# VectorE's order around the rotation of k and q: sums of exponentials moved beside the third norm's root, that norm's transpose moved behind k's cosines

## The chip, the cores and the metric

The kernel runs on one core of a Trainium2 chip. The metric is the device time in microseconds of one execution, lower is better; the time given for the kernel before is a median of 3 runs. A profile is one execution recorded by the hardware profiler. Its times are counted from the first instruction of the span. The engines are called PE (TensorE, the matrix engine; PEld are its weight loads), DVE (VectorE), ACT (ScalarE), POOL (GpSimd) and SP (SyncE, which here only issues DMAs).

## The reference, cut to what matters

Sixteen batch rows `b` of 128 positions by 512 features go through three residual blocks, all in float32:

```python
x = x + xattn(layernorm(x), ctx)      # ctx: 16 x 2048 x 512
x = x + attn(layernorm(x), ...)       # 16 heads of 32, causal, rotary
x = x + ffn(layernorm(x), Wr, A, Bw)  # + x's norm; 8 low-rank experts, top 2

def xattn(h, c):
    p = softmax(einsum('bld,bvd->blv', h, c), axis=-1)
    return einsum('blv,bvd->bld', p, c)

# in attn, for q and k of each head (the rotated half of each):
rot = stack((-x2, x1), axis=-1).reshape(x.shape)   # neighbours swapped, one negated
return x * cos + rot * sin
...
scores = where(causal, q @ k.T * scale, -inf); att = softmax(scores); y = (att @ v) @ Wc
```

The denominator of the first softmax is a sum over the 2048 context positions of the exponentials; the kernel makes it in pieces on VectorE.

## The kernel before

One batch row is one unit of work, and one pass of the loop `for b in range(B - 2)` (line 1134) works on several rows at once: it finishes the self-attention of row b (`inner`), does the experts of row b - 1 (`experts`), the scores of row b + 2 (`score`) and the weighted sum over the context of row b + 1 (`attend`). Each of these is a generator; `step(kind, b, n)` runs it to its next n `yield`s. So the order of `step` calls and the places of `yield` decide in which order instructions are issued.

Three things set the final order. PE's matmuls and all loads on a queue keep the program's order (`matmul`, `transpose`, `load`, lines 138 to 147). Instructions wrapped in `pinned` (line 151) keep it too, on their engine. The rest is placed by a scheduler when the program is built.

The stretch that the change touches lies around the rotation of k and q:

- `output` and `added` (lines 750 to 761) make the product `o` on PE and the new residual `x2` on VectorE, in the last step of `inner(b)`. There `layernorm(x2, "3_b")` (line 775) is called: `bn_stats` (tile `st`), `bn_aggr` (tile `mv`), the root on GpSimd (tile `rs`, two small instructions: add eps, then power), and the normalised `h` on VectorE (`norm_pieces`, line 186).
- `transposed` (line 263) turns `h` in blocks of 32 by 32 on VectorE into `blocks`; `send` writes them to DRAM (`there`) and `fetch` reads them back as `hT`, both on SP's queue. For the third norm this happens in the first step of `experts`, and its fetch is followed on that queue by the send and fetch of the first norm of another row.
- `rotated(n, t)` (line 653), for k and then q: `products` on PE; `shuffled` on VectorE, which swaps neighbours from PSUM into `kP` or `qP` (one tile in SBUF, tag `partner`, is used in turn by both); `sines` on GpSimd, which multiplies that tile by a table; `cosines` on VectorE, PSUM times a table, into `kT` or `qT`. `turned` (line 649) then adds the two on VectorE. `blocked` copies kT twice on ScalarE into `kb`. `compare` (line 673) multiplies qT by kb on PE, into the tiles called `pss_sc` and `pss_acc`.
- `score(b + 1)` (line 394) makes the sums of its exponentials meanwhile: `sums = sc0 + sc1`, then `+ sc2`, `+ sc3` (128 x 512 each), then `halved` (line 427), a fold of 128 x 256 and one of 128 x 128, then `across` (line 377), which begins with a transpose (`turned_den`) and ends as the reciprocal `rden`.

On PE the order of one pass around this place is: o of row b, k and q of row b + 1, one quarter of `av` (the weighted sum of row b + 2), `pss_sc`, `pss_acc`, the other three quarters, the scores `psc`, the experts' `mid` and `ffn`, then y, v and the next o.

Of the kernel before, what the change touches and what calls it, by code (L numbers as in the profile page):

```python
# [15 lines left out]
ALU = mybir.AluOpType  # L16
# [9 lines left out]
VC = V // 512  # L26
# [63 lines left out]
def perceiver_block(ctx: ExitStack, tc: tile.TileContext, io: dict, out: bass.AP):  # L90
# [60 lines left out]
    def pinned(ins):  # L151
        if not closing:
            tc.keep_in_program_order(ins)
# [55 lines left out]
    def layernorm(src, name, mix=False):  # L209
        h, pieces = norm_pieces(src, name, mix=mix)  # L210
        for piece in pieces:
            ins = piece()

            if ins is not None and name.startswith("1_") and piece is not pieces[1]:
                pinned(ins)
        return h
# [46 lines left out]
    def transposed(src, dst, name, by_tensor):  # L263
        n = src.shape[1] // P
        if by_tensor:
            for piece in tensor_pieces(lambda: src, dst, name, n):
                piece()
        else:
            blocks = p1.tile([P, 4, n, QD], F32, tag=f"blocks_{name[0]}", name=f"blocks_{name}")
            vector.transpose(blocks, src.rearrange("p (n q i) -> p q n i", n=n, q=4))  # L270
            ways[name] = blocks, dst


# [58 lines left out]
    scores, firsts, values, lasts, routes = {}, {}, {}, {}, {}  # L332
# [61 lines left out]
    def score(b):  # L394

        hT = p1.tile([P, 4, KC, QD], F32, tag="hT1" if b != 1 else "hT3", name=f"hT1_{b}")
        if b:
            h = layernorm(xs[b], f"1_{b}", mix=b == 1)
            yield
            transposed(h[:], hT, f"1_{b}", b == 1)  # L400
        else:
            first_norm(xs[b], hT)
            yield
        yield

        sc = p2.tile([P, VC, 4, S], F32, tag="sc", name=f"sc_{b}")
        mx = p1.tile([P, 4, S], F32, tag="mx", name=f"mx_{b}")
        for v, ct in enumerate(turned_cts.pop(b)):
            ps = bank(ps_sc, "sc", f"psc_{b}_{v}").rearrange("p (j t) -> p j t", j=4)
            for j in range(4):  # L410

                if v == VC - 1 and j == 3:
                    yield
                for c in range(KC):
                    matmul(
                        ps[:, j, :].rearrange("p (a i) -> p a i", a=4),
                        ct[:, c, j * P : (j + 1) * P], hT[:, :, c, :],
                        start=(c == 0), stop=(c == KC - 1),
                    )
            scalar.copy(sc[:, v], ps)  # L420

            if v:
                vector.tensor_tensor(mx, ps, mx if v > 1 else sc[:, 0], ALU.max)
            if v < VC - 1:
                yield

        def halved(t, op):
            vector.tensor_tensor(t[:, :2], t[:, :2], t[:, 2:], op)
            vector.tensor_tensor(t[:, 0], t[:, 0], t[:, 1], op)
            return t[:, 0]  # L430

        most = halved(mx, ALU.max)
        if b > 1:

            spread = p1.tile([P, 4, QD], F32, tag="spread", name=f"spread_{b}")
            peak = across(most, f"m_{b}", ALU.max, negate=True)
            for a in range(4):
                pinned(vector.transpose(
                    spread[a * QD : (a + 1) * QD], peak[:, :, None].to_broadcast([QD, 4, QD])
                ))  # L440
            for v in range(VC):
                pinned(vector.tensor_tensor(
                    sc[:, v], sc[:, v],
                    spread.rearrange("p j i -> p (j i)")[:, None, :].to_broadcast([P, 4, S]), ALU.add,
                ))
                if v < 2:
                    scalar.activation(sc[:, v], sc[:, v], AF.Exp)
            yield

            for v in range(2, VC):  # L450
                pinned(scalar.activation(sc[:, v], sc[:, v], AF.Exp))
            sums = p1.tile([P, 4, S], F32, tag="sums", name=f"sums_{b}")
            if b == B - 1:
                part = p2.tile([P, S], F32, tag="part", name=f"part_{b}")
                scores[b] = (sc, part)
                yield
                yield
                pinned(vector.tensor_tensor(sums, sc[:, 0], sc[:, 1], ALU.add))
                yield
                for v in range(2, VC):  # L460
                    pinned(vector.tensor_tensor(sums, sums, sc[:, v], ALU.add))
                named(
                    b, fold=lambda: vector.tensor_tensor(sums[:, :2], sums[:, :2], sums[:, 2:], ALU.add),
                    last_fold=lambda: vector.tensor_tensor(part, sums[:, 0], sums[:, 1], ALU.add),
                )
                yield
                return
            pinned(vector.tensor_tensor(sums, sc[:, 0], sc[:, 1], ALU.add))
            yield
            for v in range(2, VC):  # L470
                pinned(vector.tensor_tensor(sums, sums, sc[:, v], ALU.add))
            yield
            whole = across(halved(sums, ALU.add), f"den_{b}", ALU.add)
            vector.reciprocal(whole, whole)
            rden = p2.tile([P, 1], F32, tag="rden", name=f"rden_{b}")
            for a in range(4):
                vector.tensor_copy(rden[a * QD : (a + 1) * QD], whole[:, a : a + 1])
            scores[b] = (sc, rden)
            yield
            yield  # L480
            return
        yield

        tr = bank(ps_tr, "tr", f"tr_m_{b}")
        transpose(tr[:, :S], most, ident)
        nm = p2.tile([P, 1], F32, tag="nm", name=f"nm_{b}")
        vector.tensor_reduce(nm, tr[:, :S], AX.X, ALU.max, negate=True)
        diag = p1.tile([P, S], F32, tag="diag", name=f"diag_{b}")
        vector.tensor_scalar(diag, ident, nm, None, ALU.mult)
        yield  # L490
        spread = bank(ps_tr, "tr", f"spread_{b}")
        matmul(spread[:, :S], ones, diag, start=True, stop=True)
        for v in range(VC):
            vector.tensor_tensor(
                sc[:, v], sc[:, v], spread[:, None, :S].to_broadcast([P, 4, S]), ALU.add
            )
            scalar.activation(sc[:, v], sc[:, v], AF.Exp)
        part = p2.tile([P, S], F32, tag="part", name=f"part_{b}")
        scores[b] = (sc, part)
        yield  # L500
        sums = p1.tile([P, 4, S], F32, tag="sums", name=f"sums_{b}")
        pinned(vector.tensor_tensor(sums, sc[:, 0], sc[:, 1], ALU.add))
        yield
        for v in range(2, VC):
            pinned(vector.tensor_tensor(sums, sums, sc[:, v], ALU.add))

        def fold():
            vector.tensor_tensor(sums[:, :2], sums[:, :2], sums[:, 2:], ALU.add)

        def last_fold():  # L510
            vector.tensor_tensor(part, sums[:, 0], sums[:, 1], ALU.add)

        fold()
        last_fold()
        yield
# [62 lines left out]
    def inner(b):  # L578
# [179 lines left out]
        x2 = Later(p2, [P, D], tag="x2", name=f"x2_{b}")  # L758

        def added():  # L760
            vector.tensor_tensor(x2[:], banks["o"], x1[:], ALU.add)

        if b < B - 2:
            parts = [
                (project, kept), (lambda: rotated("k", kT),),
                (lambda: turned("k", kT), blocked), (lambda: rotated("q", qT),),
                (lambda: turned("q", qT),), (lambda: compare(0), lambda: compare(1)),
            ]
            parts += [(lambda group=group: weigh(group),) for group in range(4)]
            parts += [(weighted, held), (output, added)]  # L770
            for part in parts:
                for piece in part:
                    piece()
                if part[-1] is added:
                    lasts[b] = (x2, layernorm(x2, f"3_{b}"))
                yield
            return

# [280 lines left out]
    def step(kind, b, n=1):  # L1059
        if not 0 <= b < B:  # L1060
            return
        if (kind, b) not in gens:
            gens[kind, b] = kind(b)
        for _ in range(n):
            next(gens[kind, b])
# [68 lines left out]
    for b in range(B - 2):  # L1134
        if b + 3 < B:
            load_x(b + 3)
        step(inner, b)
        step(experts, b - 1)
        send(f"3_{b - 1}")
        fetch(f"3_{b - 1}")  # L1140
# [1 line left out]
            send(f"1_{b + 2}")  # L1142
            fetch(f"1_{b + 2}")
        step(inner, b, 3)
        step(score, b + 1, 2)
        step(attend, b + 1)
        step(inner, b)
        step(attend, b + 1)
# [29 lines left out]
        step(score, b + 3)  # L1178
        step(inner, b)
        step(score, b + 2)  # L1180


    y, z = B - 2, B - 1
# [60 lines left out]
```

## Time and profile before

| what | us |
|---|---|
| median of 3 runs (812.15 to 812.86) | 812.8 |
| the profiled execution, whole time | 812.06 |
| its span, first to last instruction | 810.3 |
| length of one pass of the loop (distance of two starts of `pss_sc`, 222.09 and 270.10) | 48.01 |
| POOL multiplying kP or qP by sines, one | 1.27 |
| VectorE, 128 x 512 float32, one (sums, cosines, additions) | 0.65 to 0.69 |
| VectorE, block transpose 128 x 512, one | 0.71 |
| mean DMA rate over the span, GB/s | 260 |

The granted TensorE clock was 1.0 throughout. How to read the timelines used below: each row is start, duration, engine, line, operation, the tile written and those read after an arrow, shapes and count; in square brackets the engine's idle time before it and whom it waited for. All instructions issued through the helpers have line L115 (vector, scalar, gpsimd), L139 (matmuls) or L147 (loads), so rows are told apart by their tiles. Consecutive instructions of one engine overlap a little in the records[...].

### The profile page before, as it was taken

To read this page: it belongs to the slowest core of one execution; us is meant where nothing else is said; L and a number is where in the kernel's file an instruction comes from. 1 tells how busy PE (TensorE), PEld (TensorE's weight loads), DVE (VectorE), ACT (ScalarE), POOL (GpSimd) and SP (SyncE) were. 2 spreads that over 40 slices of the span, in tenths; PEclk is the share of its full clock that TensorE was granted. 3 is DMA by queue.
4 is the path that set the end of the run, shared out by engine and by line. 5 is a ranking of instruction groups with operands and counts; after the bars stand their busy time and mean duration, and the time that the engine had idled before them with its cause. 6 is when DMAs were issued, how large, how long until landed. Compare 5 with 4: busy or idle time off the path is not lost.

```text
span 810.3 us, 14522 instructions
## 1 busy us (share of the span) xinstructions
PE 790.0 (98%) x5444; PEld 559.8 (69%) x5444; DVE 612.2 (76%) x1593; ACT 258.2 (32%) x772; POOL 146.4 (18%) x214
## 2 busy tenths in 40 slices
PE   9999999999999999999999999999999999999996
PEld 9946775768677586866758677576867757686554
DVE  2464779686886968789696878968688696866785
ACT  2232324232232413223241232423223241322452
POOL 1001010212111121211212121021211112121204
PEclk9999999999999999999999999999999999999999
DMA  9997394867949588593957859486794948755102
GB/s 374 417 395 313 121 382 166 333 259 237 373 145 373 198 299 323 189 403 138 360 228 287 332 171 399 168 313 262 251 365 148 381 182 321 288 194 209 40 2 79
DMA packets 76870, 211.06 MB, mean 260 GB/s; under 512 B 6400, under 2 KB 42624, under 8 KB 60416
## 3 DMA queue, kind: packets, MB, share of 16 engines
q10 hardware_dynamic: 15696, 113.32, 35.1%
q1 hardware_dynamic: 57168, 84.75, 29.3%
q0 software_dynamic: 3936, 12.07, 4.5%
q8 instruction: 43, 0.70, 0.3%
q14 instruction: 27, 0.22, 0.1%
HBM read 180.23 MB, written 29.88 MB: 259 GB/s over the span
## 4 chain that ended last, share of the span: by engine, by line
PE 79%; DVE 13%; POOL 4%; issue 3%; DMA 0%; POOLq 0%; ACT 0%; DVEq 0%
PE psc L139 28%; PE av L139 22%; PE v L139 7%; PE o L139 7%; DVE sums L115 2%; PE pss_sc L139 2%; POOL qP L115 2%; DVE kT L115 2%; PE y L139 2%; PE pss_acc L139 2%; PE ffn L139 2%; PE mid L139 2%; POOL rs L115 1%; PE k L139 1%; PE q L139 1%
## 5 line engine op out<-in xcount | busy, mean ns | idle before, releaser
L139 PEld LDWEIGHTS psc<-hT,ctxT 128*128 128x128 f32 x2048 | 232.3, 192 | 6.7 <-issue 3.6
L139 PE MATMUL psc<-hT,ctxT 128*128 128x128 f32 x2048 | 233.9, 275 | 0.0
L139 PE MATMUL av<-ctx,sc 128*128 128x512 f32 x512 | 227.3, 596 | 0.0
L139 PEld LDWEIGHTS av<-ctx,sc 128*128 128x128 f32 x512 | 94.4, 190 | 110.5 <-issue 110.5
L115 ACT ACTIVATE att<-att,nmx 128x128 f32<-128x128 f32 x256 | 99.3, 389 | 77.5 <-DVE nmx L115 75.7
L115 POOL TENSOR_SCALAR rs<-mv 128x1 f32<-128x1 f32 x47 | 10.6, 225 | 411.8 <-DVE g_top L115 217.6
L115 ACT COPY sc<-psc 128x512 f32<-128x512 f32 x64 | 37.3, 582 | 120.3 <-PE psc L139 120.3
L115 ACT ACTIVATE kb<-kT,cst 128x512 f32<-128x512 f32 (+1 forms) x34 | 36.1, 1111 | 109.7 <-DVE kT L115 109.7
L115 DVE TENSOR_SCALAR h<-x,mv,rs 128x512 f32<-128x512 f32 x47 | 26.6, 567 | 54.5 <-POOL rs L115 54.5
L139 PEld LDWEIGHTS k<-hT,w_k 128*128 128x128 f32 x512 | 59.6, 192 | 8.2 <-issue 7.5
L115 ACT ACTIVATE sc<-sc 128x512 f32<-128x512 f32 x64 | 38.2, 627 | 69.9 <-DVE sc L115 56.0
L139 PE MATMUL k<-hT,w_k 128*128 128x128 f32 x512 | 60.1, 275 | 0.0
L139 PE MATMUL q<-hT,w_q 128*128 128x128 f32 x512 | 60.0, 275 | 0.0
L139 PE MATMUL o<-w_c,yT 128*128 128x512 f32 x128 | 59.2, 605 | 0.0
L139 PE MATMUL v<-w_v,hT 128*32 128x512 f32 x520 | 59.0, 593 | 0.0
L139 PEld LDWEIGHTS q<-hT,w_q 128*128 128x128 f32 x512 | 58.5, 192 | 0.0
L115 ACT ACTIVATION_READ_ACCUMULATOR att<-att,nmx 128x1 f32 x256 | 47.9, 187 | 0.0
L139 PEld LDWEIGHTS o<-w_c,yT 128*128 128x128 f32 x128 | 23.0, 189 | 35.5 <-issue 34.7
L115 DVE TENSOR_TENSOR mx<-psc,mx 128x512 f32<-128x512 f32 x32 | 21.6, 675 | 33.5 <-ACT sc L115 33.5
L115 DVE TENSOR_TENSOR att<-att,rsm 128x512 f32<-128x512 f32 x64 | 43.4, 678 | 0.7
L115 DVE TENSOR_REDUCE nmx<-att 128x4 f32<-128x512 f32 x64 | 43.1, 675 | 1.0
L115 DVE TENSOR_TENSOR sc<-sc,spread 128x512 f32<-128x512 f32 x64 | 40.0, 686 | 3.8 <-PE spread L139 3.3
(157 smaller groups left out, 898.8 us busy)
## 6 DMA issues: line engine op xcount, KB each, us to landing
ctx<-in_ctx_dram ACTq DMA_DIRECT2D x56, 1024.0 KB, 9.6
ctxT<-in_ctxT_dram ACTq DMA_DIRECT2D x52, 1024.0 KB, 9.8
there_p<-pX SPq DMA_DIRECT2D x28, 512.0 KB, 3.5
pT<-there_p SPq DMA_DIRECT2D x28, 512.0 KB, 4.4
ctxT<-in_ctxT_dram SPq DMA_DIRECT2D x12, 1024.0 KB, 9.0
there<-blocks SPq DMA_DIRECT2D x42, 256.0 KB, 3.4
hT<-there SPq DMA_DIRECT2D x42, 256.0 KB, 3.1
ctx<-in_ctx_dram SPq DMA_DIRECT2D x8, 1024.0 KB, 10.5
```

What stands on the lines that cost most here:

```text
L115: ins = issue(*args, **kwargs)
L139: tc.keep_in_program_order(nc.tensor.matmul(*args, **kwargs))
```

## The change

The arithmetic and the instructions stay; their order on VectorE changes. In `score`, the sum of the third quarter moves up to the first, the fourth stands alone, and the two folds get a step of their own ahead of `across`. In the last step of `inner`, h of the third norm is put off: statistics and root are issued, then comes a `yield`, and h follows in an added step at the end of the pass. The transpose of h is pinned, and one step of `score(b + 1)` moves ahead of `experts(b - 1)`, so that the folds stand ahead of that transpose.

```diff
@@ transposed
-            vector.transpose(blocks, src.rearrange("p (n q i) -> p q n i", n=n, q=4))
+            turn = vector.transpose(blocks, src.rearrange("p (n q i) -> p q n i", n=n, q=4))
+            if name[0] == "3":
+                pinned(turn)
@@ score
             pinned(vector.tensor_tensor(sums, sc[:, 0], sc[:, 1], ALU.add))
-            yield
-            for v in range(2, VC):
-                pinned(vector.tensor_tensor(sums, sums, sc[:, v], ALU.add))
-            yield
-            whole = across(halved(sums, ALU.add), f"den_{b}", ALU.add)
+            pinned(vector.tensor_tensor(sums, sums, sc[:, 2], ALU.add))
+            yield
+            pinned(vector.tensor_tensor(sums, sums, sc[:, 3], ALU.add))
+            yield
+            part = halved(sums, ALU.add)
+            yield
+            whole = across(part, f"den_{b}", ALU.add)
...
-            yield
             yield
             return
@@ inner
-            vector.tensor_tensor(x2[:], banks["o"], x1[:], ALU.add)
+            pinned(vector.tensor_tensor(x2[:], banks["o"], x1[:], ALU.add))
...
-                    lasts[b] = (x2, layernorm(x2, f"3_{b}"))
+                    h, norm = norm_pieces(x2, f"3_{b}")
+                    for piece in norm[:3]:
+                        piece()
+
+                    yield
+                    pinned(norm[3]())
+                    lasts[b] = x2, h
                 yield
@@ the loop over b
         step(inner, b)
+        step(score, b + 1)
         step(experts, b - 1)
...
         step(inner, b, 3)
-        step(score, b + 1, 2)
+        step(score, b + 1)
         step(attend, b + 1)
...
         step(score, b + 2)
+        step(inner, b)
```

On VectorE the order of a pass (from the second on) becomes, as the program is built:

```
before: sums(0+1) x st mv h blocks sums+2 sums+3 kP kT=cos fold256 kT+=kP fold128 qP qT=cos turned_den qT+=qP ...
after:  sums(0+1) x st mv sums+2 sums+3 h kP kT=cos fold256 fold128 blocks kT+=kP qP qT=cos qT+=qP turned_den ...
```

In the pass b = 1 the sum (0+1) stands between h and blocks before, and between mv and sums+2 after. In the pass b = 0 the sum (0+1) stands behind the addition into qT before, and between k's cosines and the addition into kT after. Behind the loop, for row 14, the transpose alone moves, from behind h to behind k's cosines. The orders on PE, ACT, POOL and SP stay as they were.

## The prediction

> **What bounds the kernel now.** I read first the page's busy shares, then the waits, then one loop of the batch loop engine by engine. TensorE (PE) is busy almost throughout:
>
> ```profile
> PE 790.0 (98%) x5444; PEld 559.8 (69%) x5444; DVE 612.2 (76%) x1593; ACT 258.2 (32%) x772; POOL 146.4 (18%) x214
> ```
>
> So only a PE stall can be won back. The list of waits names one that recurs:
>
> ```profile
> PE pss_sc L139 <- DVE qT L115: 11.1, 13, 1.3
> DVE qT L115 <- POOL qP L115: 10.4, 15, 0.9
> ```
>
> PE waits 13 times, 11.1 us in all, for VectorE's (DVE's) last step on qT, and that step waits for GpSimd (POOL). PE's timeline of one loop (start, length, work, idle before) shows where:
>
> ```profile
> 258.55 3.73 PE L139 MATMUL k<-hT,w_k 128*128 128x128 f32 x32
> 262.12 3.74 PE L139 MATMUL q<-hT,w_q 128*128 128x128 f32 x32
> 265.69 3.60 PE L139 MATMUL av<-ctx,sc 128*128 128x512 f32 x8
> 270.10 0.70 PE L139 MATMUL pss_sc<-kb,qT 64*128 64x256 f32 x4 [0.81 <-DVE qT L115]
> ```
>
> k, q and a quarter of av fill PE until 269.29; qT is late by 0.81. Loops 2 to 13 show 0.81 to 0.84 each, loop 1 shows 1.28; there is no other PE gap in those loops. Now VectorE and GpSimd in that loop:
>
> ```profile
> 260.20 0.18 DVE L115 BATCH_NORM_AGGREGATE mv<-st 128x2 f32<-128x6 f32 x1
> ...
> 261.39 0.55 DVE L115 TENSOR_SCALAR h<-x,mv,rs 128x512 f32<-128x512 f32 x1 [1.01 <-POOL rs L115]
> 261.97 0.71 DVE L115 STREAM_TRANSPOSE blocks<-h 128x512 f32<-128x512 f32 x1
> 262.61 1.44 DVE L115 TENSOR_TENSOR sums<-sums,sc 128x512 f32<-128x512 f32 x2
> ...
> 263.98 0.73 DVE L115 STREAM_SHUFFLE kP<-k 128x512 f32<-128x512 f32 x1
> ...
> 265.19 1.15 DVE L115 TENSOR_TENSOR sums<-sums 128x256 f32<-128x256 f32 x1
> ...
> 266.26 0.68 DVE L115 TENSOR_TENSOR kT<-kT,kP 128x512 f32<-128x512 f32 x1
> ...
> 267.07 0.74 DVE L115 STREAM_SHUFFLE qP<-q 128x512 f32<-128x512 f32 x1
> ...
> 269.26 0.69 DVE L115 TENSOR_TENSOR qT<-qT,qP 128x512 f32<-128x512 f32 x1 [0.67 <-POOL qP L115]
> ```
> ```profile
> 260.48 0.22 POOL L115 TENSOR_SCALAR rs<-mv 128x1 f32<-128x1 f32 x1 [6.35 <-DVE mv L115]
> 260.79 0.57 POOL L115 TENSOR_TENSOR rs<-rs,mhalf 128x1 f32<-128x1 f32 x1
> 264.78 1.27 POOL L115 TENSOR_TENSOR kP<-kP,cst 128x512 f32<-128x512 f32 x1 [3.43 <-DVE kP L115]
> ```
>
> The reader is to see four things. VectorE idles 1.01 while GpSimd makes the norm's root (rs). k is ready on PE at 262.28, but its shuffle starts at 263.98, behind transpose and sums. The 128x256 fold takes 1.15, though the same shape took 0.42 at 251.15 (mx): it ends 0.28 after GpSimd's sines on kP (266.06), so the two collided. From kP's shuffle on, everything is a chain into qT.
>
> **The change, step by step, in this loop.** In the new order the sums of the exponentials stand between mv and h; then h, kP, cosines, both folds, blocks, the add into kT, qP, its cosines, the add into qT, and only then turned_den. No instruction is added or removed.
>
> *1. Sums beside the root.* The aggregate starts at 260.20; an independent instruction follows 0.10 behind the start of one (at 786.69 and 786.79). So the first sum runs 260.30 to 260.99 (0.69). If GpSimd worked beside it untouched, the root would be done at 261.36, and h would follow the sums. But one place of the trace has such a pair:
>
> ```profile
> 786.97 0.72 DVE L115 TENSOR_TENSOR att<-att,rsm 128x512 f32<-128x512 f32 x1
> ...
> 787.26 0.85 POOL L115 TENSOR_TENSOR rs<-rs,mhalf 128x1 f32<-128x1 f32 x1
> ```
>
> The power, elsewhere 0.57, took 0.85 and ended 0.43 after VectorE's instruction with two SBUF operands (787.69 to 788.11). So about 0.14 of a blocked GpSimd instruction still overlaps. I take that row: the addition of eps ends at 260.99 + 0.22 - 0.14 = 261.07. The second sum begins 0.10 after the first (as it does before), 261.09 to 261.78; the power ends 0.43 later, 262.21; h starts at 262.25; kP's shuffle 0.46 behind (h at 116.87, the next at 117.33): 262.71, after PE's k. That is **1.27 earlier** than 263.98. Bounds: no collision, h at 261.70 and kP at PE's 262.31, 1.67 earlier; eps missing the 0.10 gap between the sums, kP at 263.02, 0.96 earlier.
>
> *2. Folds and transpose ahead of the add into kT.* Before, that add starts 2.28 after kP's shuffle. Now: 0.81 to GpSimd's start, 1.27 its work, 0.28 to the end of the 128x256 fold, 0.04 gap, 0.20 for the 128x128 fold, 0.64 for blocks (its distance to the next instruction at 261.97) = 3.24. **0.96 later.** The wait for GpSimd was no free time for the fold: it cannot end sooner, and only then come fold and transpose. This is the dear part of the change.
>
> *3. qP.* It started 0.81 behind that add's start, with the small fold between; now only the add's 0.68 and a gap of 0.04: **0.09 earlier**. PE's q (265.86) is ready.
>
> *4. turned_den behind qT.* It lay in the wait for GpSimd's qP and was free; qT still waits for GpSimd, 2.19 after qP's start. So qT moves as qP does. The masks come at qT + 2.83 rather than + 2.51, 0.32 later against PE. Cover: VectorE idles 1.87 before mx at 242.39, and PE's mid starts 0.44 to 3.6 after wa is copied. Cost 0; without cover at most 0.32 a loop.
>
> *5. SyncE's queue.* The third norm's send needs blocks, now done at 266.02 for 262.68, 3.3 later; behind it stand its fetch, the next first norm's send and fetch. If all slip by 3.3, hT for g_share lands at 277.2 (needed at 279.58) and hT for psc at 281.0 (needed at 282.0). Cost 0 with 1.0 left; beyond that, us for us. kb on ScalarE (2.37) ends at 269.1, before qT. GpSimd's queue holds nothing else there.
>
> *6. Ends.* Loop 0: the first sum falls into kP's window and the add into kT slips 0.47, but qP waits for PE's q anyway: 0. Loop 14: the transpose fits the 0.82 wait for GpSimd, and qP waits for PE's q: 0. x's add keeps its place: 0.
>
> **Sum:** 1.27 - 0.96 + 0.09 = 0.40 a loop; PE's gap falls from 0.81 to 0.41. Loop 1, with three sums in that place, I put at 0.4 too. 13 x 0.40 = **5.2 us**: the profiled execution of 812.06 (span 810.3) becomes 806.9, the median of 812.8 **807.6**.
>
> **Rule against row.** The Trainium skill, "SBUF — State Buffer", section "Who interferes with whom", says a VectorE instruction with two SBUF inputs contends with GpSimd reading SBUF, and that the second to issue fully blocks until the first has finished. It speaks against this change. Taken whole, the loser would pay its full length after the winner: the fold 0.42 behind GpSimd rather than the row's 0.28 (0.145 dearer), eps ending at 261.21, the second sum at 261.90, the power at 262.47, kP at 262.97 (1.01 earlier): 1.01 - 0.96 - 0.145 + 0.09 = 0, and the time stays. By the rows it is 0.40. Both collisions in the trace (0.28 for 0.42, 0.43 for 0.57) show the blocked instruction overlapping its first 0.14; I follow them.
>
> **Rivals.**
> - *A, no collision at the root.* For: a 128x1 operand is read quickly. Against: the row at 787.26. Gain 1.67 - 0.96 + 0.09 = 0.80, the whole stall: 13 x 0.80 = 10.4, 802.4.
> - *B, the gain is eaten.* The rule's sum, or eps missing the gap (0.96 - 0.96 + 0.09): about 812.
> - *C, slower, by the collision in full.* Place: kP's shuffle and the fold. eps misses the gap (the two sums run on to 261.78), both its 0.22 and the power's 0.57 follow undiminished with 0.08 between, h at 262.69, kP at 263.15 (0.83 earlier), and the fold pays 0.42: 0.83 - 0.96 - 0.145 + 0.09 = -0.19; 13 x 0.19 = 2.4, 815.2. It decides from the point where kP's shuffle gains less than 0.87, that is starts after 263.11. For: three added meetings on one interface. Against: eps has waited since 260.48 when the gap opens.
>
> **Numbers.** Forecast 45%, own range 0.2 to 0.6 a loop (805.0 to 810.2); A 20%, B 20%, C 15%. About 0.2% (1.6 us) is what a measurement tells from no change: faster 0.65, same 0.20, slower 0.15. Range 802.0 to 813.6: A's end below, B's upper side above, C left out.
>
> **What would show it.** Right: PE's wait for qT near 0.4 in 13 loops, the power lengthened from 0.57 to about 1.0, kP's shuffle 1.3 earlier against o's end, the 128x256 fold again near 1.15, the add into kT 1.2 behind GpSimd's end rather than 0.2. Wrong: a power of 0.57 beside the sums (A); kP's shuffle under 0.9 earlier (B, C); a new PE gap before psc or mid, which would mean the slipped sends or the late masks.

## The result and the profile after

The changed kernel takes 808.18 us (median of 22 runs) against 813.25 us for the kernel before, run beside it: a ratio of 0.9946, 95% interval 0.9923 to 0.9968. That is 5.1 us; 5.2 had been forecast (807.6 us against a median of 812.8). The profiled execution took 808.20 us, its span 806.4. Most executions of both kernels list a granted clock of 0.998 over the span, the profiled one after too; the profiled one before lists 1.0, as 5 of 39 further executions of that kernel do, and is about 1 us below its median.

The same views as before. The page's busy shares, and two lines of the list of waits (engine, line, what was waited for: us in all, times, longest):

```profile
PE 791.7 (98%) x5444; PEld 561.1 (70%) x5444; DVE 615.3 (76%) x1593; ACT 258.3 (32%) x772; POOL 156.8 (19%) x214
```
```profile
PE pss_sc L139 <- DVE qT L115: 5.6, 12, 0.7
...
DVE qT L115 <- POOL qP L115: 13.2, 15, 0.9
```

PE's wait for qT has halved, from 11.1 to 5.6 us. GpSimd is busy 156.8 us instead of 146.4 with the same 214 instructions: its two small instructions for the root are now held up in each of the 13 loops, as the rows below show. One loop on PE, then on VectorE, then on GpSimd:

```profile
264.59 3.60 PE L139 MATMUL av<-ctx,sc 128*128 128x512 f32 x8
268.63 1.13 PE L139 MATMUL pss_sc<-kb,qT 64*128 64x256 f32 x8 [0.44 <-DVE qT L115]
```
```profile
259.10 0.18 DVE L115 BATCH_NORM_AGGREGATE mv<-st 128x2 f32<-128x6 f32 x1
259.20 1.46 DVE L115 TENSOR_TENSOR sums<-sums,sc 128x512 f32<-128x512 f32 x2
261.12 0.55 DVE L115 TENSOR_SCALAR h<-x,mv,rs 128x512 f32<-128x512 f32 x1 [0.46 <-POOL rs L115]
...
261.58 0.73 DVE L115 STREAM_SHUFFLE kP<-k 128x512 f32<-128x512 f32 x1
...
262.80 1.48 DVE L115 TENSOR_TENSOR sums<-sums 128x256 f32<-128x256 f32 x2
264.19 0.70 DVE L115 STREAM_TRANSPOSE blocks<-h 128x512 f32<-128x512 f32 x1
264.82 0.65 DVE L115 TENSOR_TENSOR kT<-kT,kP 128x512 f32<-128x512 f32 x1
...
267.79 0.69 DVE L115 TENSOR_TENSOR qT<-qT,qP 128x512 f32<-128x512 f32 x1 [0.88 <-POOL qP L115]
```
```profile
259.38 0.56 POOL L115 TENSOR_SCALAR rs<-mv 128x1 f32<-128x1 f32 x1 [6.35 <-DVE mv L115]
260.02 1.05 POOL L115 TENSOR_TENSOR rs<-rs,mhalf 128x1 f32<-128x1 f32 x1
262.39 1.27 POOL L115 TENSOR_TENSOR kP<-kP,cst 128x512 f32<-128x512 f32 x1 [1.32 <-DVE kP L115]
```

The reader is to see both sides of the bargain. The wait for the root shrank from 1.01 to 0.46 us because the sums fill it, but they stretch the root itself: the addition of eps takes 0.56 instead of 0.22, the power 1.05 instead of 0.57, each ending just behind a sum. And GpSimd's sines on kP are done at 263.67, yet the addition into kT starts only at 264.82: the folds and the transpose stand between. PE's gap is 0.44 instead of 0.81, and one pass of the loop takes 47.64 instead of 48.01.

From the first pss_sc to that of row 13 the profiled execution gained 5.3 us (79.11 to 702.41 before, 79.36 to 697.38 after). Of this, 0.25 were lost in the matmuls ahead of the loop and 1.1 in the closing part, which the last section comes back to.

### The profile page after: what moved, and what is told of

Read it like the earlier page. It is cut to its first block, busy times and chain, and to the rows that moved or that the text cites. A ratio compares the mean times of both kernels' runs of the same rounds, so it can differ in the third digit from the quotient of the medians.

```text
span 806.4 us, 14497 instructions
## 1 busy us (share of the span) xinstructions
PE 791.7 (98%) x5444; PEld 561.1 (70%) x5444; DVE 615.3 (76%) x1593; ACT 258.3 (32%) x772; POOL 156.8 (19%) x214
## 4 chain that ended last, share of the span: by engine, by line
PE 78%; DVE 14%; POOL 5%; issue 1%; DMA 1%; ACT 1%; DVEq 0%; POOLq 0%; ACTq 0%
PE psc L139 27%; PE av L139 21%; PE v L139 7%; PE o L139 7%; POOL rs L115 2%; DVE sums L115 2%; PE pss_sc L139 2%; POOL qP L115 2%; PE y L139 2%; PE k L139 2%; PE ffn L139 2%; PE q L139 2%; DVE kT L115 2%; PE pss_acc L139 2%; PE mid L139 2%
## 5 line engine op out<-in xcount | busy, mean ns | idle before, releaser
L115 POOL TENSOR_SCALAR rs<-mv 128x1 f32<-128x1 f32 x47 | 14.6, 311 | 416.0 <-DVE g_top L115 222.1
```

Of the source, the lines that this page charges most:

```text
L115: ins = issue(*args, **kwargs)
```

## The experiments

The theory: a VectorE instruction with two operands in SBUF and an instruction of GpSimd hold each other up where they meet. The sums beside the root are the gain; folds and transpose ahead of the addition into kT are a cost. The rivals: the transpose's move is the gain, or folds and transpose are free where they stand, since GpSimd is awaited anyway. All kernels below differ from the changed one in VectorE's order, and two of them by one added instruction; the orders on PE, POOL and SP stay the same, and ACT's too but for one kernel, where it is said. The cuts from their edits leave out how the folds and turned_den are split into steps and pinned; where the loop over b is edited in the first and the last experiment, its first pass (b = 0) is left in the order of the kernel before.

**1. The sums alone.** The transpose goes back ahead of k's shuffle, the folds to either side of the addition into kT, for which `score` yields after each of these steps.

```diff
...
-        step(inner, b)
-        step(score, b + 1)
         step(experts, b - 1)
+        step(inner, b)
...
-        step(inner, b, 3)
-        step(score, b + 1)
+        step(score, b + 1); step(inner, b)   # fold of 256; addition into kT
+        step(score, b + 1); step(inner, b)   # fold of 128; q's shuffle and cosines
+        step(score, b + 1); step(inner, b)   # turned_den; addition into qT
+        step(score, b + 1)                   # the rest of the denominators
```

> Half of the change: the sums stay beside the root, the transpose goes back ahead of k's shuffle and the two folds back to either side of the addition into kT. Collision theory (what lies between GpSimd's sines on kP and the addition into kT is dear, the sums beside the root are the gain): k's shuffle starts 0.54 earlier than before (h 2.0 after mv, then 0.58 and 0.64 for the transpose), the addition into kT again 0.2 behind GpSimd's end; PE's gap before pss_sc 0.27 instead of 0.45 with the whole change and 0.81 before; about 806 us, faster than the whole change by 2. Rival (the transpose's move is what gains, the sums are indifferent): gap near 0.8, about 813.

Measured: 805.44 us (6 runs), ratio to before 0.9911 (0.9888 to 0.9934); PE's gap 0.26 to 0.29 in eleven of the twelve loops from the second on, 0.38 in one. In the list of waits:

```profile
PE pss_sc L139 <- DVE qT L115: 4.0, 13, 0.5
```

The addition into kT starts 0.20 behind GpSimd's sines again. Half of the change is worth more than the whole.

**2. The transpose and the folds alone.** The sums go back behind h.

```diff
             pinned(vector.tensor_tensor(sums, sc[:, 0], sc[:, 1], ALU.add))
+            yield
             pinned(vector.tensor_tensor(sums, sums, sc[:, 2], ALU.add))
-            yield
             pinned(vector.tensor_tensor(sums, sums, sc[:, 3], ALU.add))
...
                     for piece in norm[:3]:
                         piece()
-
-                    yield
                     pinned(norm[3]())
...
-        step(inner, b)
```

> The other half: the sums go back behind h, the transpose stays behind k's cosines and both folds. Collision theory: k's shuffle 0.64 earlier than before, the addition into kT 0.96 later behind it, qP 0.09 nearer: gap 0.81 + 0.23 = 1.05, about 816 us, slower than before. Rival (the wait for GpSimd's sines hides folds and transpose): gap near 0.1, about 804.

Measured: 815.97 us (10 runs), ratio 1.0065 (1.0033 to 1.0097); gap 1.00 to 1.03 in loops 2 to 13.

```profile
PE pss_sc L139 <- DVE qT L115: 14.0, 13, 1.8
```

This half alone makes the kernel slower. The two halves nearly add up: the gap falls by 0.54 with the first, rises by 0.20 with the second, and falls by 0.37 with both. The rival that has the transpose as the gain falls, and so does the one that has the wait for GpSimd as free time. Experiments 4 and 5 take folds and transpose apart.

**3. One instruction more ahead of the sums.** In one loop of the changed kernel, the twelfth, PE's gap was only 0.13. There VectorE's first sum was issued 0.19 later than in the other loops (0.29 behind mv's start instead of 0.10; the profile puts this wait down to ScalarE's work on sc):

```profile
640.81 1.51 DVE L115 TENSOR_TENSOR sums<-sums,sc 128x512 f32<-128x512 f32 x2
642.24 0.54 DVE L115 TENSOR_SCALAR h<-x,mv,rs 128x512 f32<-128x512 f32 x1
```
```profile
640.81 0.22 POOL L115 TENSOR_SCALAR rs<-mv 128x1 f32<-128x1 f32 x1 [5.84 <-DVE mv L115]
641.11 0.85 POOL L115 TENSOR_TENSOR rs<-rs,mhalf 128x1 f32<-128x1 f32 x1
```

Here eps was 6 ns ahead of the sum, and took its usual 0.22; h came 1.72 behind mv's start instead of 2.02. So the order of issue was to be forced:

```diff
                         piece()
+                    if 0 < b:
+                        least = p2.tile([P, 1], F32, tag="least", name=f"least_{b}")
+                        pinned(vector.tensor_reduce(least, cst[:, :144], AX.X, ALU.max))
 
                     yield
```

> The whole change, with one more VectorE instruction, a reduction of 128x144 constants with one SBUF operand, between mv and the sums (from the second loop on), so that GpSimd's addition of eps is issued ahead of the first sum. Collision theory (who is issued first has the read interface): eps takes 0.22 instead of 0.56, the power about 0.85 instead of 1.05, h starts 1.75 behind mv instead of 2.0; gap 0.18 instead of 0.45; about 804.7 us, although work is added. Rival (the root is late for a reason of its own): the sums and h are 0.2 to 0.3 later, gap about 0.7, about 811.5.

Measured: 809.85 us (14 runs), ratio 0.9971 (0.9949 to 0.9993), gap 0.65 to 0.67 in loops 2 to 13: the rival's side. But the trace shows that the reduction did not let eps through:

```profile
259.99 1.48 DVE L115 TENSOR_TENSOR sums<-sums,sc 128x512 f32<-128x512 f32 x2
```
```profile
259.99 0.77 POOL L115 TENSOR_SCALAR rs<-mv 128x1 f32<-128x1 f32 x1 [6.34 <-DVE mv L115]
```

The two starts lie 2 ns apart in the record (259.989 on GpSimd, 259.991 on VectorE), and GpSimd lost: 0.77. In loops 2 to 13 eps is 2 to 6 ns ahead by the record, and loses each time. In one of them (594.963 against 594.969) it is ahead by 6 ns, as in the loop of the changed kernel where it won. So starts this close do not tell who goes first, and the run decides nothing: the margin of 0.03 us that I had reckoned with was too thin. It was repeated with 256 columns.

> The whole change with a reduction of 128x256 constants instead of 128x144 between mv and the sums. In the run with 128x144 the first sum was issued 2 ns after GpSimd's addition of eps and still went first; in the one loop of the whole change where eps was 6 ns ahead, eps took 0.22. The longer reduction puts the first sum 0.42 behind mv's start, 0.14 behind eps. Collision theory: eps 0.22, the power about 0.97 and ending 0.43 behind the first sum, h bound by the sums at 1.83 behind mv instead of 2.0; gap 0.26; about 805.8 us. Rival (an added instruction only delays the root and the sums): gap 0.75 or more, about 812.

Measured: 805.2 us (6 runs), ratio 0.9919 (0.9894 to 0.9943), gap 0.21 to 0.23 in loops 2 to 13:

```profile
258.50 0.39 DVE L115 TENSOR_REDUCE least<-cst 128x1 f32<-128x256 f32 x1
258.80 1.48 DVE L115 TENSOR_TENSOR sums<-sums,sc 128x512 f32<-128x512 f32 x2
260.20 0.54 DVE L115 TENSOR_SCALAR h<-x,mv,rs 128x512 f32<-128x512 f32 x1
```
```profile
258.68 0.22 POOL L115 TENSOR_SCALAR rs<-mv 128x1 f32<-128x1 f32 x1 [6.35 <-DVE mv L115]
258.99 0.93 POOL L115 TENSOR_TENSOR rs<-rs,mhalf 128x1 f32<-128x1 f32 x1
```

With eps 0.12 ahead it takes 0.22, the power (0.93, still longer than its 0.57 alone) ends while the second sum runs, and h no longer waits for GpSimd. The reduction has one operand in SBUF; it ran beside eps and did not lengthen it. So the kernel with an instruction added on the critical stretch is 3 us faster than the changed one (805.2 against 808.18), and what it changed in the trace is the order of eps and the first sum.

**4. The folds behind the addition into qT.** Only the transpose stays beside GpSimd's sines on kP.

```diff
...
         step(inner, b)
-        step(score, b + 1)
         step(experts, b - 1)
...
         step(inner, b, 3)
-        step(score, b + 1)
+        step(score, b + 1, 2)
         step(attend, b + 1)
```

> The whole change, but with both folds behind the addition into qT, so that only the transpose lies beside GpSimd's sines on kP. Collision theory: the addition into kT 0.04 behind GpSimd's end instead of 1.15, qP's shuffle waits for PE's q, qT is ready before PE asks: gap 0; loop 47.2 instead of 47.64; about 802.4 us. Rival (the fold was free where it stood, since GpSimd was awaited anyway): gap stays near 0.45 and the later masks cost something: 808 or more.

Measured: PE's gap before pss_sc is gone in all 13 loops, and a pass takes 47.12 us. The addition into kT starts 0.03 behind the end of GpSimd's sines. So the transpose alone costs nothing there; it is dear where it stands behind the folds, which end only after the sines (the addition then comes 1.15 behind them, and with the fold of 256 alone, as before, 0.20). But the time is worse than with the change: median 814.49, from 803.43 to 826.11 in 22 runs; the lower 15 of them have a median of 810.07, a ratio to before of 0.9971 (0.9949 to 0.9993). The profiled execution (span 806.3) shows a new wait, on PE, and the fetch it waits for on SP's queue beside the ctx loads on ACT's:

```profile
201.47 1.08 PE L139 MATMUL y<-pT,vv 128*32 128x128 f32 x32
206.88 6.15 PE L139 MATMUL v<-w_v,hT 128*32 128x512 f32 x32 [4.34 <-DMA hT<-there]
```
```profile
195.80 0.37 SPq L147 DMA_DIRECT2D hT<-there  x1
```
```profile
196.31 1.97 ACTq L147 DMA_DIRECT2D ctx<-in_ctx_dram  x4
```

In this loop the fetch of hT for v, 256 KB, was issued 0.5 us ahead of four loads of 1 MB each, and landed after 10.9 us. In the other loops of this kernel the same fetch landed after 4.1 to 5.4 (where the profile has its landing); the 2.9 in the expectation below is a median over all fetches of hT in a stretch of the kernel before. PE waited 4.34; v itself then took 6.15 instead of 3.62. The pass took 54.2. The fetch is late because VectorE is: the masks start 2.5 us behind pss_sc, against 1.67 before and 2.02 with the change, and what follows up to the transpose ahead of this fetch is an almost solid row of VectorE work, while the ctx loads follow PE. The lead of this fetch over the ctx loads in loops 1 to 13 is 1.3 to 2.8 us before, 1.5 to 2.3 with the change, 0.5 to 2.0 here. So the kernel with the folds last was run with the ctx loads behind the experts' gating on ACT's queue. This also moved two instructions in VectorE's order (the experts' last addition comes earlier, and the first sum, which stood ahead of x, now follows mv) and one copy on ACT (of v, ahead of two exponentials):

```diff
-        load_ctx(b + 2)
         step(score, b + 2)
         step(experts, b - 1)
+        load_ctx(b + 2)
         step(score, b + 2)
```

> The kernel with the folds last, but its four ctx loads issued behind the experts' gating on ScalarE's queue, some 3.5 us later. With the folds last, one loop had PE waiting 4.3 us for hT before v: its fetch was issued 0.5 us ahead of the ctx burst and took 10.9 us instead of 2.9. If the burst is the cause: no such wait, gap 0, about 802.5 us with little spread. If the fetch is late for another reason (VectorE's later masks alone): waits at v of some us remain in some loops, 806 to 820.

Measured: 801.46 us (801.12 to 802.42, 4 runs), ratio 0.9861 (0.9846 to 0.9875), no wait at v, lead 3.7 to 5.6. So in this kernel the place of the ctx loads decides: with them later, the wait and the spread are gone. That the executions without a profile lost their time in the same wait is inferred. And a short lead alone is not enough for it. In one loop of the kernel with the longer reduction the same fetch was as close ahead of the burst,

```profile
195.65 0.37 SPq L147 DMA_DIRECT2D hT<-there  x1
```
```profile
196.18 1.95 ACTq L147 DMA_DIRECT2D ctx<-in_ctx_dram  x4
```

and landed after 3.6 us, without a wait. What has to come on top of a short lead stays open.

**5. The folds where nobody else works.** Between the addition into kT and q's shuffle VectorE waits for PE's q, and GpSimd is idle.

```diff
...
         step(inner, b)
-        step(score, b + 1)
         step(experts, b - 1)
...
-        step(inner, b, 3)
-        step(score, b + 1)
+        step(inner, b); step(score, b + 1)   # addition into kT; both folds
+        step(inner, b); step(score, b + 1)   # q's shuffle and cosines; turned_den
+        step(inner, b); step(score, b + 1)   # addition into qT; the rest
         step(attend, b + 1)
```

> The whole change, but the two folds stand between the addition into kT and q's shuffle, where VectorE waits for PE's q and GpSimd is idle, and the denominators' first transpose stands in the wait for GpSimd's qP, as before. Collision theory: fold of 128x256 in 0.42, not 1.15; q's shuffle 0.25 behind PE's q, qT 0.8 earlier than with the whole change: gap 0 in every loop. The masks come 1.5 behind pss_sc's start instead of 2.0, so that the third fetch (hT for v) keeps a lead of 2.5 us or more over the burst of ctx loads: no stall at v, about 802.4 us with little spread, faster than both kernels. Rival (removing PE's gap itself sets off stalls elsewhere): 806 to 826 as with the folds last.

Measured: **801.34 us** (800.75 to 802.06, 4 runs), ratio 0.9856 (0.9841 to 0.9871), with the ctx loads where they were. VectorE, GpSimd and PE in one loop:

```profile
261.02 0.70 DVE L115 STREAM_TRANSPOSE blocks<-h 128x512 f32<-128x512 f32 x1
261.93 0.69 DVE L115 TENSOR_TENSOR kT<-kT,kP 128x512 f32<-128x512 f32 x1 [0.20 <-POOL kP L115]
262.54 0.74 DVE L115 TENSOR_TENSOR sums<-sums 128x256 f32<-128x256 f32 x2
```
```profile
260.62 1.28 POOL L115 TENSOR_TENSOR kP<-kP,cst 128x512 f32<-128x512 f32 x1 [1.31 <-DVE kP L115]
```
```profile
262.81 3.60 PE L139 MATMUL av<-ctx,sc 128*128 128x512 f32 x8
266.34 1.14 PE L139 MATMUL pss_sc<-kb,qT 64*128 64x256 f32 x8
```

Both folds together take 0.74, where beside the sines they took 1.48; the transpose, which has one operand, hides behind the sines: neither is lengthened by the other (0.70 and 1.28, elsewhere 0.71 and 1.27). pss_sc follows av with no idle time in loops 2 to 13, and with 0.08 in loop 1. The masks start 1.6 behind pss_sc. In another point too the expectation was off: the fetch's lead is 1.2 to 2.8, not 2.5 or more in every loop; no wait at v came of it. This kernel beats both the kernel before and the changed one.

## Why the prediction was right

Each row counts from the event named (forecast in the loop shown before, measured in the loop shown after).

| step | forecast | measured |
|---|---|---|
| 1: eps's end behind mv's start | 0.87 | 0.84 |
| 1: power's end, same | 2.01 | 1.98 |
| 1: k's shuffle, same (before 3.77) | 2.51 | 2.49 |
| 2: addition into kT behind k's shuffle (before 2.28) | 3.24 | 3.23 |
| 3: q's shuffle behind that addition (before 0.81) | 0.72 | 0.78 |
| 3: addition into qT behind q's shuffle | 2.19 | 2.19 |
| PE's gap before pss_sc (before 0.81) | 0.41 | 0.44 |

- *Step 1* held to a few hundredths, because it was built on the one place of the trace where a power on GpSimd met a VectorE instruction of two SBUF tiles. Rival A, no collision, falls: eps took 0.56 and the power 1.05, and even with eps ahead of the sums, in the kernel with the longer reduction, the power took 0.93 and not 0.57.
- *Step 2*, called the dear part, held as well (0.95 against the 0.96 forecast). The half-change without the sums shows it alone: the gap is 0.20 wider than before. The sum is right for this order only: the transpose costs its 0.64 because it stands behind the folds, and without them it fits into the wait (0.03, experiment 4).
- *Step 3* was off by 0.06: the addition into kT took 0.65, and q's shuffle started 0.13 behind its end, not 0.04. Steps 1 and 2 gave back 0.03 of it, which leaves the 0.03 by which the gap was forecast too small.
- *Step 4*: the masks came 0.35 later against PE (forecast 0.32) and cost nothing here. But the cover that I named was the wrong one. The lead of the fetch of hT for v over the ctx loads, which I counted nowhere, shrank too (experiment 4); with the folds last it was down to 0.5 in one loop of the profiled execution, and that loop cost 7 us.
- *Step 5*: the third norm's send was issued at 264.93, its fetch at 271.43 and the first norm's fetch at 275.33. Against pss_sc this is 2.0 later than before for both fetches, not the 3.3 that I allowed for; psc did not wait.
- *Step 6*: loop 0 as forecast (the first sum took 1.41 in the sines' window, and qT was not later). Loop 1 was put at 0.4 and gained 0.60 (1.28 to 0.68).
- *Rule against row*: the rule of the Trainium skill, "SBUF — State Buffer", section "Who interferes with whom", says the right thing of who blocks whom, and its sentence that the order of issue decides is what the longer reduction shows (eps 0.22 when it is 0.12 ahead, 0.56 when it is 0.18 behind). Taken as a price it gave a gain of 0; the overlap of about 0.14 that the row showed recurs in each blocked instruction of the new trace (eps ends 0.085 behind the first sum instead of 0.22, the power 0.42 behind the second instead of 0.57), and the row was the better basis.

The sum was 13 x 0.40 = 5.2, and the loops gave 5.3. In part this is luck: eleven gaps fell by 0.36 to 0.40, but the first by 0.60. The twelfth fell by 0.69, but its pass is no shorter than the others, since PE lost 0.31 there earlier, at mid, whose weights (wa) came late; and in the kernel before one pass was 0.15 longer than the rest. The medians differ by 5.1. The two profiled executions differ by 3.9, since in the one after the head and the closing part took 1.4 back.

## What to carry to other kernels

When VectorE's work is moved into a time in which GpSimd works, look at the trace for a place where the two kinds of instruction already meet, and take both lengths from there; here a wait for GpSimd was free room only for instructions that did not meet it. Put the work that does meet it where GpSimd is idle: here this was worth another 7 us, more than the change itself. And when one engine's work moves against that of the bounding engine, transfers that follow the two move against each other as well: check the leads of small transfers over large ones, not only the waits.

## What the runs showed that was not expected

- Who of two engines goes first is worth 0.34 to 0.55 us for an instruction of 0.22 (eps), and the recorded starts do not tell it when they lie within 6 ns: eps went first in one such loop and had to wait in twelve. An instruction added in front, which set the starts 0.12 apart, made the kernel 3 us faster.
- Part of the closing stretch ran at a granted clock of one half. PE waits about 2.5 us before mid in both kernels; behind it the granted clock was 1.00 before, and with the change 0.50 for a while. The matmuls of ffn took 1.02 before and 1.91 after:

```profile
800.59 1.16 PE L139 MATMUL mid<-hT,wa 128*128 128x128 f32 x8 [2.48 <-POOL wa L115]
...
802.88 1.02 PE L139 MATMUL ffn<-wb,mid 128*128 128x512 f32 x2
```
```profile
795.55 1.16 PE L139 MATMUL mid<-hT,wa 128*128 128x128 f32 x8 [2.47 <-POOL wa L115]
...
798.25 1.91 PE L139 MATMUL ffn<-wb,mid 128*128 128x512 f32 x2
```

The clock of these stretches, before and after (stretch and length, busy us and instructions of PE, PEld, DVE, ACT and POOL, granted clock, DMA share, GB/s):

```profile
801.00:806.00 5.00, 3.81 (x23) 2.58 (x23) 2.53 (x3) 1.32 (x3) 2.74 (x3) 1.00 0.27 96
```
```profile
798.00:800.00 2.00, 2.00 (x6) 0.92 (x5) 0.92 (x1) 0.59 (x1) 1.38 (x2) 0.50 0.40 131
```

This accounts for the 1.1 us that the closing part lost. In the kernel with the folds last, v ran at 0.50 after its wait of 4.34 us, but behind the wait of 2.48 before mid the clock stayed at 1.00, as it did in the kernel before. So a wait of this length does not settle it by itself; why the clock fell in one execution and not in another was not tried.
